# A state-space layer and a mixture-of-experts attention layer: gate products ahead of their Silus, sums with the newest state last, the first outputs further back

## The chip, the cores and the metric

The kernel is one program on one core of a Trainium2 chip. The metric is the device time of one execution in microseconds; the median of the runs counts. All times below that are places in the execution are microseconds from the start of the profiled span.

The engines have short names in the profile. PE is the matmul engine, with PEld its weight loads. DVE is the vector engine, ACT the scalar engine, POOL the GpSimd engine and SP the engine that issues most transfers. Each engine works through its own instructions in the order in which the program put them there; an instruction that waits holds up all behind it on that engine.

## The reference

The input is x with 8 sequences of 512 tokens and 256 features, in float32. Two layers follow one another, each as `x + layernorm(layer(layernorm(x)))`.

The first layer is a state-space layer (Mamba) with 512 inner channels and 16 states per channel:

```python
xz = x @ in_proj_w.T
x_ssm, z = jnp.split(xz, 2, axis=-1)
xc = silu(causal_conv(x_ssm, conv_w) + conv_b)      # 4 taps per channel
xp = xc @ x_proj_w.T                                # 1 + 16 + 16 columns
dt = softplus(dt_r @ dt_proj_w.T + dt_proj_b)
h = dA_t * h + dBx_t                                # a scan over the 512 tokens
y = einsum('bdn,bn->bd', h, C_t)                    # summed over the 16 states
return (y + xc * D) * silu(z) @ out_proj_w.T
```

The second layer is an attention with 16 heads of 64 features, in which the values and the outputs of every head are sums over 8 experts. A sigmoid gate per head and expert keeps the best two of the eight. A feed-forward part with 1024 hidden features and two layer norms follow:

```python
v = einsum('bsd,bhse,hedp->bhsp', x, gate(x, Wsel_v), Wv)
att = softmax(q @ k.T / 8)                          # q, k with rotary angles
o = einsum('bhst,bhtp->bhsp', att, v)
src2 = einsum('bhsp,bhse,hepd->bsd', o, gate(x, Wsel_o), Wo)
```

## The kernel before

**Names.** b is the sequence (0 to 7), a pair is two heads, so there are eight pairs (0 to 7) per sequence. The page's line numbers are those of the file; all DVE instructions stand at L175, because a helper issues them, so they are told apart by the names of their tiles.

**Order.** PE, DVE, ACT and POOL take their instructions in the order in which the Python code emits them (L1274); SP's transfers are placed by the framework. The code decides this order with a small planner, `_Order` (L98-162). It keeps a clock `now` for PE, which `pe(us)` moves on by a declared cost, and a clock `vec` for DVE. `after(us, do)` puts a piece of work in a queue with a due time. Background routines are generators: each `yield wait` says when the routine may go on, and a part of one is emitted when DVE has room in the plan. `order_of.run()` emits all that is due by `now`, and `order_of.run(until)` moves the clock on until a condition holds. So the declared costs set the order of the instructions but not their times.

**The routines.** `front(b)` does the input side of the state-space layer of sequence b: norm, input projection, convolution, Silu, the projection to step size and states, the gate silu(z), which is kept in DRAM (`sz_d`). `mamba(b)` does the scan and the output side, and then the gates of the attention's values (`best(0, gv)`); at the end it starts `heads(b)`, which does the gates of the outputs (`best(1, gt)`), turns them on PE into `ps_go`, copies them, stores them in `go_d` and adds b to the set `gated` (L781-795). `feed_forward(b)` is what follows the attention.

**The scan.** A step k (0 to 31) treats two of the 16 states (NG = 2) for 128 of the 512 channels (block m = k mod 4). DVE makes a scan over 2 x 512 elements and then the product of h with ct, the C coefficients. ACT computes the decay `da` for step k + 1 during step k. From step 4 of sequence 0 on, PE makes the scan's inputs as matmuls with diagonal matrices, in a PSUM tile `ps_u`; those for step k + 1 are emitted at step k (L643). POOL adds the products to `xc` by accumulating transfers, two per step (`add`, L570). The last four steps of sequence 0 are added by PE instead: `add_last` (L578) sums the two states of h and xc in PSUM with the identity as weights, and DVE multiplies two blocks at a time with the gate (L673). The number of the step last begun is kept in `at["step"]`.

**The second front.** `front(1)` runs during the scan of sequence 0. When step 8 (2 x NC) has begun it emits two gate products, `ps_in_g` and `ps_in` (L401, L402), each with its weight transfer on SP, then the Silus of xs, then the Silus and stores of the two gates (L404, L411), and 2.2 us later the state projection `ps_x`. The two products lie in PSUM until ACT has read them.

**The attention.** `ahead(n, following)` (L1257) emits PE's order for a pair n, mixed with the outputs of the pair before it. "v0" is a value product (`values`, two token blocks for one head), "s0" a block of scores (`scores`), "t0" the turning of a softmax block (`turn_over`), a number is an output product of the pair before (`add_output`), and `following` the next pair's projection to q and k. Behind a value product DVE forms ve, with the gates, and POOL sums over experts. Behind scores DVE takes the maximum (low), ACT the exponentials, DVE a reciprocal (total), and ACT scales. Value products, scores and turned blocks take three PSUM buffers in turn (`banks`, L282).

`attend` (L939) multiplies softmax and values, copies the result to `o`, and asks for the first two output gates 0.8 and 0.9 us later in the plan (`weigh_soon`, L956): if b is in `gated`, `weigh` is called, else it asks again 0.5 us later. `weigh` (L963) issues the transfers of the gate rows (`gb`, from `go_d`) on SP and the product og on DVE. There are two buffers each for gb and og. Output products k = 2q and 2q + 1 read og q; after the second one, `weigh(q + 2)` is emitted (L1006).

Of the kernel before, what the change touches and what calls it, by code (L numbers as in the profile page):

```python
# [37 lines left out]
NC = DI // P  # L38
NG = 2
# [58 lines left out]
class _Order:  # L98
# [11 lines left out]
    def pe(self, us):  # L110
        self.now += us
        self.here = self.now
# [4 lines left out]
    def after(self, us, do):  # L117

        heapq.heappush(self.queue, (self.here + us, self.n, do))
        self.n += 1  # L120
# [95 lines left out]
def _layers(  # L216
# [4 lines left out]
    with ExitStack() as ctx:  # L221
# [8 lines left out]
        step = pool("step", 2)  # L230
# [51 lines left out]
        def banks(name):  # L282
            return psum.tile([P, 2, S], F32, tag="mm", name=name)
# [14 lines left out]
        n = NT * 2 * H  # L298
        steps = NS // NG * NC

        at = dict(step=-1)
        state = {}
        pe, after, then = order_of.pe, order_of.after, order_of.then

        def front(b):
# [34 lines left out]
            def project(m, ps=None):  # L340

                w = wpool.tile([P, ND, 2 * P], F32, tag="w_m", name=f"w_in_{b}_{m}")
                nc.sync.dma_start(out=w, in_=m_in[:, :, m * P : (m + 2) * P])
                ps = banks(f"ps_in_{b}_{m}") if ps is None else ps
                for i in range(2):
                    for c in range(ND):
                        nc.tensor.matmul(  # L347
                            ps[:, i, :], lhsT=w[:, c, bass.ts(i, P)], rhs=xt[:, c, :],
                            start=(c == 0), stop=(c == ND - 1),
                        )  # L350
                pe(3.42)
                return ps
# [24 lines left out]
            for m in range(NC):  # L377
# [7 lines left out]
                for k in range(KC - 1):  # L385
                    yield 0.0
                    late = KC - 1 - k
# [7 lines left out]
                    states(px, range(2))  # L395
                    pe(1.71)
            yield free(0.1)
            while b == 1 and at["step"] < 2 * NC:
                yield Free(0.5)
            if b == 1:  # L400
                gates = [project(NC, psum_a.tile([P, 2, S], F32, tag="sum", name="ps_in_g"))]  # L401
                gates.append(project(NC + 2))  # L402
            for xc in xs if b else xs[1:]:
                nc.scalar.activation(xc, xc, AF.Silu)  # L404
            if b == 0:
# [66 lines left out]
            for u in us:  # L472
                m = 2 * len(lns)
# [11 lines left out]
            for ln, u in zip(lns, us):  # L485
                m = 2 * lns.index(ln)
# [13 lines left out]
        def mamba(b):  # L500
# [67 lines left out]
            xc = one.tile([P, NC, S], F32, tag="xc", name=f"xc_{b}")  # L568
# [9 lines left out]
            def add_last(k):  # L578

                m, h = k % NC, hs[k]  # L580
                if m % 2 == 0:
                    last.append(
                        banks("ps_y") if m else psum_a.tile([P, 2, S], F32, tag="sum", name="ps_y_0")
                    )
                terms = [h[:, j, :] for j in range(NG)] + [xc[:, m, :]]
                for i, a in enumerate(terms):
                    nc.tensor.matmul(
                        last[-1][:, m % 2, :], lhsT=ident, rhs=a,
                        start=(i == 0), stop=(i == len(terms) - 1),
                    )  # L590
                pe(2.6)

            scanning.add(b)
            if b + 1 < B:
                if b:
                    order_of.start(front(b + 1), 2 * b - 1 if b > 1 else 2.5)
                order_of.start(mamba(b + 1), 2 * (b + 1))
# [5 lines left out]
            for k in range(steps):  # L603
                g, m = k // NC * NG, k % NC
# [12 lines left out]
                h = hs[k] = step.tile([P, NG, S], F32, tag="h", bufs=4, name=f"h_{b}_{k}")  # L617
# [30 lines left out]
                if k - 1 >= by_dma:  # L648
                    add_last(k - 1)
# [14 lines left out]
            if b:  # L664
                yield 5.2
                add(steps - 1, 1)
                yield 3.5
            else:
                add_last(steps - 1)
                yield 0.1  # L670
# [126 lines left out]
        class Pair:  # L797
# [155 lines left out]
                for q in range(E // 2 if self.final else 2):  # L953
                    after(0.8 + 0.1 * q, lambda q=q: self.weigh_soon(q))

            def weigh_soon(self, q):  # L956

                if self.b in gated:
                    self.weigh(q)
                else:  # L960
                    after(0.5, lambda: self.weigh_soon(q))

            def weigh(self, q):  # L963

# [292 lines left out]
        def ahead(n, following):  # L1257


            for part in (  # L1260
                "v0", "s0", 0, 1, "v1", "s1", 2, 3, "t0", "s2", "v2", "t1", "s3", following, 4,
                "v3", 5, "t2", 6, "t3", 7,
            ):
                if isinstance(part, int):
                    if last:
                        last.add_output(part)
                elif isinstance(part, str):
                    {"v": n.values, "s": n.scores, "t": n.turn_over}[part[0]](int(part[1]))
                else:
                    part()  # L1270
                order_of.run()

        last, net = None, last_net()
        with tc.manual_schedule(engines=MANUAL):  # L1274
            first = front(0)
            order_of.start(first, 0, next(first))
            order_of.start(mamba(0), 0)
            order_of.start(front(1), FIRST, 9.0)
            first_constants()
            order_of.run(lambda: 0 in scanning)  # L1280
            order_of.start(later_constants(), NET)
            load(0, 0)
            order_of.run(lambda: 0 in inputs_of)
            pairs = {}
            follow(-1, H // 2 - 1)
            for b in range(B):
                for pair in range(H // 2):
                    if (b, pair) == (B - 1, 1):
                        next(net)
                    now = pairs.pop((b, pair))  # L1290
                    load(*next_one(b, pair))
                    ahead(now, lambda: follow(b, pair))
                    if pair == 0 and b:
                        order_of.start(feed_forward(b - 1, sums[b - 1]), NET)
                    now.attend()
                    order_of.run()
                    last = now
            order_of.run(lambda: not order_of.rest)
            next(net, None)
# [83 lines left out]
```

## Time and profile before

| what | us |
|---|---|
| median of 3 runs (lowest to highest) | 3668.6 (3666.76 to 3671.24) |
| the profiled execution's own time | 3673.76 |
| its span, first to last instruction | 3672.0 |
| PE busy (11250 matmuls) | 3406.9 (93%) |
| DVE busy | 3048.9 (83%) |
| ACT busy | 1664.0 (45%) |
| POOL busy | 1677.5 (46%) |
| mean granted PE clock, share of full | 0.97 |

The page divides the span into 40 slices of 91.8 us; a digit is the busy share of one slice in tenths, and PEclk is the PE clock that was granted. In the timeline a row is a start, a duration, the engine, the line, the operation, what it writes and reads, shapes and count; the bracket at the end gives how long the engine stood idle before it and what released it. Rows of like instructions are merged, so a row's duration can hold gaps. Some matmul records are missing from a trace.

### The profile page before, as it was taken

How to read it: one execution, taken by the hardware profiler on the slowest of the kernel's cores; microseconds unless marked ns; L12 is line 12 of the kernel's file. 1: busy time of each engine (PE TensorE's matmuls, PEld its weight loads, DVE VectorE, ACT ScalarE, POOL GpSimd, SP SyncE). 2: the span in 40 equal slices, each digit the busy share in tenths (PEclk: the TensorE clock that was granted, in tenths of full speed). 3: DMA queues.
4: the chain of work that ended last, by engine and by line, in shares of the span. 5: the costliest groups of instructions: out<-in, count | busy, mean ns of one | idle time of the engine just before them, and what ended most of it. 6: DMA issues, size and time to landing. Idle time of an engine off the chain costs nothing.

```text
span 3672.0 us, 35171 instructions
## 1 busy us (share of the span) xinstructions
PE 3406.9 (93%) x11250; PEld 1678.2 (46%) x11250; DVE 3048.9 (83%) x3198; ACT 1664.0 (45%) x2866; POOL 1677.5 (46%) x1597
## 2 busy tenths in 40 slices
PE   5768989989899999999999999999999999999997
PEld 3533334444344444444444444445444444446555
DVE  7878898799989898999989998899988999654443
ACT  5624443545543455344644446444553444332332
POOL 1425663354645545354454555355443657232321
PEclk8879999999999999999999999999999999999999
DMA  4927774577866768577755868568765778443430
GB/s 136 198 73 175 179 173 115 150 181 176 196 144 165 176 169 195 124 182 181 197 139 143 203 154 204 146 154 188 183 171 128 181 186 203 118 126 92 115 106 26
DMA packets 282534, 574.06 MB, mean 156 GB/s; under 512 B 37224, under 2 KB 124520, under 8 KB 282096
## 3 DMA queue, kind: packets, MB, share of 16 engines
q1 hardware_dynamic: 201584, 422.88, 40.0%
q0 software_dynamic: 80768, 148.95, 24.3%
q8 instruction: 91, 1.49, 0.2%
q14 instruction: 91, 0.75, 0.1%
HBM read 403.36 MB, written 19.42 MB: 115 GB/s over the span
## 4 chain that ended last, share of the span: by engine, by line
PE 48%; DVE 27%; issue 8%; DMA 7%; ACT 5%; POOL 5%; SPq 0%; DVEq 0%; POOLq 0%; ACTq 0%
PE ps_v L916 14%; DVE h L175 11%; PE ps_a L1000 9%; DMA xc<-h 5%; PE ps_qk L819 5%; PE ps_s L857 4%; PE ps_a L1020 3%; PE ps_o L946 3%; PE ps_pt L892 3%; DVE ve L175 2%; DVE og L175 2%; DVE low L175 2%; DVE xs L175 2%; PE ps_in L347 1%; DVE hit L175 1%
## 5 line engine op out<-in xcount | busy, mean ns | idle before, releaser
L916 PE MATMUL ps_v<-wv,xt 128*128 128x512 f32 x2048 | 945.8, 605 | 20.4 <-DVE y L175 13.3
L932 POOL TENSOR_TENSOR ve<-ve 128x512 f32<-128x512 f32 x256 | 423.6, 1655 | 1148.1 <-DVE ve L175 996.5
L1000 PE MATMUL ps_a<-og,wo 128*128 128x512 f32 x1792 | 847.1, 606 | 28.0 <-DVE og L175 27.7
L872 ACT ACTIVATE p<-ps_s,low 128x512 f32<-128x512 f32 x512 | 347.3, 683 | 723.0 <-DVE low L175 722.6
L574 POOL DMA_DIRECT2D xc<-h x504 | 463.8, 1099 | 382.1 <-DMA xc<-h 170.0
L916 PEld LDWEIGHTS ps_v<-wv,xt 128*128 128x128 f32 x2048 | 385.9, 193 | 536.9 <-issue 481.3
L175 DVE TENSOR_TENSOR_SCAN h<-da,h 128x1024 f32<-128x1024 f32 x228 | 541.2, 2374 | 10.3 <-ACT da L511 0.4
L1000 PEld LDWEIGHTS ps_a<-og,wo 128*128 128x128 f32 x1792 | 326.5, 192 | 440.9 <-issue 371.4
L881 ACT ACTIVATE p<-p,total 128x512 f32<-128x512 f32 x512 | 341.5, 714 | 252.2 <-DVE total L175 251.4
L175 DVE TENSOR_TENSOR og<-o,gb 128x1024 f32<-128x1024 f32 x256 | 320.1, 1271 | 128.8 <-ACT o L952 81.6
L175 DVE TENSOR_TENSOR ve<-ps_v,gv 128x1024 f32<-128x1024 f32 x256 | 311.7, 1218 | 130.0 <-PE ps_v L916 102.7
L898 ACT COPY pt<-ps_pt 128x1024 f32<-128x1024 f32 x256 | 256.9, 1005 | 347.3 <-PE ps_pt L892 345.9
L511 ACT ACTIVATE da<-dt,decay 128x511 f32<-128x511 f32 x512 | 339.8, 714 | 103.9 <-DVE h L175 100.8
L175 DVE TENSOR_TENSOR h<-bt,dtx 128x1024 f32<-128x1024 f32 x228 | 321.2, 1409 | 34.6 <-DMA xc<-h 34.4
L175 DVE TENSOR_TENSOR h<-h,ct 128x1024 f32<-128x1024 f32 x256 | 338.0, 1320 | 3.8
L175 DVE TENSOR_REDUCE low<-ps_s 128x2 f32<-128x1024 f32 x256 | 310.8, 1214 | 26.8 <-PE ps_s L857 26.1
L933 POOL TENSOR_TENSOR ve<-ve 128x256 f32<-128x256 f32 x256 | 318.1, 1243 | 20.1
L841 POOL DMA_DIRECT2D qk<-sin x256 | 204.5, 1209 | 256.7 <-DVE qk L175 128.9
L857 PE MATMUL ps_s<-qk 64*128 64x512 f32 x1024 | 295.0, 650 | 24.3 <-ACT p L872 14.0
L892 PEld LDWEIGHTS ps_pt<-ident,p 128*128 128x128 f32 x2048 | 239.4, 141 | 124.1 <-issue 87.1
L946 PE MATMUL ps_o<-pt,v 128*64 128x512 f32 x1024 | 249.9, 615 | 30.8 <-POOL v L934 16.7
L892 PE MATMUL ps_pt<-ident,p 128*128 128x128 f32 x2048 | 266.8, 274 | 6.4 <-ACT pt L898 2.6
(165 smaller groups left out, 3579.0 us busy)
## 6 DMA issues: line engine op xcount, KB each, us to landing
gb<-go_d SPq DMA_DIRECT2D x512, 256.0 KB, 4.8
xc<-h POOLq DMA_DIRECT2D x504, 256.0 KB, 5.6
wv<-in_wv_dram SPq DMA_DIRECT2D x128, 512.0 KB, 5.9
wo<-in_wo_dram SPq DMA_DIRECT2D x504, 128.0 KB, 4.0
ct<-bc_d SPq DMA_DIRECT2D x64, 512.0 KB, 5.8
bt<-bc_d SPq DMA_DIRECT2D x57, 512.0 KB, 5.6
wqk<-in_wqk_dram SPq DMA_DIRECT2D x64, 256.0 KB, 2.7
qk<-sin POOLq DMA_DIRECT2D x256, 64.0 KB, 4.8
```

The costliest lines, as they stand in the source:

```text
L175: return getattr(self.engine, name)(*args, **kw)
L511: nc.scalar.activation(das[k % 2][:, j, 1:S], dt[:, m, 1:S], AF.Exp, scale=decay[:, m, g + j : g + j + 1],)
L574: nc.gpsimd.dma_start(out=xc[:, k % NC, :], in_=hs[k][:, j, :], accum_op=ALU.add)
L857: nc.tensor.matmul(ps[:, j, :], lhsT=self.qk[feats, 0, bass.ts(t, P)], rhs=self.qk[feats, 1, :], start=True, stop=True,)
L872: nc.scalar.activation(p[:, j, :], ps[:, j, :], AF.Exp, bias=low[:, j : j + 1], accum_out=total[:, j : j + 1],)
L881: nc.scalar.mul(p[:, j, :], p[:, j, :], total[:, j : j + 1])
L892: nc.tensor.transpose(pp[:, j, bass.ts(i, P)], self.p[t][:, j, bass.ts(i, P)], ident)
L916: nc.tensor.matmul(ps[:, i, :], lhsT=self.xt[:, c, bass.ts(t + i, P)], rhs=self.wv[:, c, :], start=(c == 0), stop=(c == ND - 1),)
L932: nc.gpsimd.tensor_tensor(ve[:, :, 0:4], ve[:, :, 0:4], ve[:, :, 4:8], ALU.add)
L933: nc.gpsimd.tensor_tensor(ve[:, :, 0:2], ve[:, :, 0:2], ve[:, :, 2:4], ALU.add)
L946: nc.tensor.matmul(po[j * HP : j * HP + HP, 0, :], lhsT=self.v[:, j, t, :], rhs=self.pt[:, j, t, :], start=(t == 0), stop=(t == NT - 1),)
L1000: nc.tensor.matmul(pa[:, c, :], lhsT=self.wo[:, i, bass.ts(c, P)], rhs=self.og[q][:, i, :], start=(self.pair == 0 and k == 0), stop=(self. ...
```

## The change

There are three edits, all effective near the start of the program.

1. In `front(1)` the two gate products are emitted when step 7 has begun, and the Silus wait until step 9 has begun.
2. In `add_last` the term xc is summed first and the two states of h after it.
3. For pair 1 of sequence 0, whose outputs are those of pair 0, PE's order is v0 s0 v1 s1 t0, then outputs 0 and 1, and then s2 v2, outputs 2 and 3, t1 s3. The other pairs keep their order. And `weigh_soon`, where it had to ask more than once, puts `weigh` into the plan 6.0 us after the gates are there.

```diff
@@ front
-            while b == 1 and at["step"] < 2 * NC:
+            while b == 1 and at["step"] < 2 * NC - 1:
                 yield Free(0.5)
             if b == 1:
                 gates = [project(NC, psum_a.tile([P, 2, S], F32, tag="sum", name="ps_in_g"))]
                 gates.append(project(NC + 2))
+                while at["step"] < 2 * NC + 1:
+                    yield Free(0.5)
             for xc in xs if b else xs[1:]:
                 nc.scalar.activation(xc, xc, AF.Silu)
@@ add_last
-                terms = [h[:, j, :] for j in range(NG)] + [xc[:, m, :]]
+                terms = [xc[:, m, :]] + [h[:, j, :] for j in range(NG)]
@@ weigh_soon
-            def weigh_soon(self, q):
+            def weigh_soon(self, q, late=False):
                 if self.b in gated:
-                    self.weigh(q)
+                    after(6.0 if late else 0.0, lambda: self.weigh(q))
                 else:
-                    after(0.5, lambda: self.weigh_soon(q))
+                    after(0.5, lambda: self.weigh_soon(q, True))
@@ ahead
-            for part in (
+            usual = (
                 "v0", "s0", 0, 1, "v1", "s1", 2, 3, "t0", "s2", "v2", "t1", "s3", following, 4,
                 "v3", 5, "t2", 6, "t3", 7,
-            ):
+            )
+            second = (
+                "v0", "s0", "v1", "s1", "t0", 0, 1, "s2", "v2", 2, 3, "t1", "s3", following, 4,
+                "v3", 5, "t2", 6, "t3", 7,
+            )
+            for part in second if (n.b, n.pair) == (0, 1) else usual:
```

## Prediction

> **What bounds the kernel now.** I read the page's slices first, then the waits of DVE and PE, then the timeline around the three places that the change touches.
>
> ```profile
> PE   5768989989899999999999999999999999999997
> DVE  7878898799989898999989998899988999654443
> PEclk8879999999999999999999999999999999999999
> ```
>
> A slice is 91.8 us. From the fourth on PE is nine tenths busy, and DVE nearly so until the last ones. Only the first three (to 275 us) have slack: there the scan of batch 0 runs on DVE. All three edits lie before 335 us. After that the program order is the old one (shown below), so a microsecond won or lost there is carried to the end; nothing later waits for a fixed time.
>
> **Part 1: the gate products (L398-411).** Timeline before:
>
> ```profile
> 93.36 4.02 PE L549 MATMUL ps_u<-diag,dtx_t 128*128 128x128 f32 x20 [2.23 <-ACT diag L539]
> 97.21 3.60 PE L347 MATMUL ps_in_g<-xt_m,w_in 128*128 128x512 f32 x8
> ...
> 104.28 1.02 ACT L364 ACTIVATE sz<-ps_in 128x1024 f32<-128x1024 f32 x1 [2.41 <-PE ps_in L347]
> ...
> 107.98 2.29 DVE L175 TENSOR_TENSOR_SCAN h<-da,ps_u 128x1024 f32<-128x1024 f32 x1 [4.71 <-ACT da L511]
> ```
>
> Scan 10 waits 4.71 us for its decay (da), which stands on ACT behind two table loads, four Silus and ACT's waits for the products (0.49 + 2.41). The change gives the products to PE behind the inputs of scan 8, and the Silus to ACT behind the decay of scan 10. ACT's 2.9 us of waiting go. But PE is in order: the inputs of scan 9 now stand behind 16 matmuls. They start at 94.2 (the last four of scan 8's inputs, from 93.36 at 0.21 each). The granted clock, read in stretches of half a microsecond, was 0.50 from 89.7 to 96.56, then 1.00. So 2.36 us at 0.86 each make 2.7 of them, and 13.3 at 0.43 take 5.7: done at 102.3. The inputs of scan 9 (16 at 0.11) end at 104.05, and scan 9, which ran at 99.74, starts at 104.1. **The stall moves from scan 10 to scan 9.** On: scan 9 to 106.4, product to 107.6, scan 10 to 109.9, product to 111.0. ACT: Silus from 100.6, over at 105.95, table 1.28, decay 11 at 108.6. PE: inputs 10 to 105.8, state projection (3.43) to 109.4, inputs 11 to 111.3. Scan 11 at 111.35 against 111.66: gain 0.3. With the clock at 1.00 throughout it would be 1.4 better on PE, with another 3.4 us at 0.50 some 1.7 worse: +-1.5. SP: the weights of the products are loaded by 45 us, so their moved DMAs cost nothing; the two stores of sz move by about 3 us and are read at 176 us. The PSUM bank of the second product is free (105.95) before the state projection takes it.
>
> **Part 2: the last states' sums (L585).** The tail of that scan:
>
> ```profile
> 187.03 2.29 DVE L175 TENSOR_TENSOR_SCAN h<-da,ps_u 128x1024 f32<-128x1024 f32 x1 [4.21 <-DMA xc<-h]
> ...
> 190.72 3.75 PE L587 MATMUL ps_y<-h,ident 128*128 128x512 f32 x4 [4.10 <-DVE h L175]
> ...
> 194.27 1.67 PE L587 MATMUL ps_y<-xc,ident 128*128 128x512 f32 x2
> 195.77 1.88 PE L587 MATMUL ps_y<-h,ident 128*128 128x512 f32 x4
> 197.49 1.02 PE L587 MATMUL ps_y<-xc,ident 128*128 128x512 f32 x2
> 198.35 1.03 PE L684 MATMUL ps_out<-w_out,xc 128*128 128x256 f32 x4
> 198.55 1.23 DVE L175 TENSOR_TENSOR xc<-ps_y,sz 128x1024 f32<-128x1024 f32 x1 [3.38 <-PE ps_y L587]
> ```
>
> With xc first, the new order waits at its head for xc's DMA adds. They are there: scan 30 at 187.03 and scan 31 at 190.50 could write their buffers only when those adds had landed. So xc of state 30 runs at 187.05, in PE's idle 4.1 us. The stop in the middle of that idle time then keeps the clock up: in this trace PE's clock fell to 0.50 at 188.73 after a stretch of 3.4 us with 38% busy, and stayed at 1.00 over one with 49% (311.6 to 315.0). Here the stretch has 55%. Then h of state 30: 190.72 to 192.6, xc of state 31 to 193.5, and h of state 31, whose product ends at 194.04, to 196.0. The DVE product follows at 196.1 against 198.55: gain 2.4. With the clock at 0.50 as before it is 1.2. I take 2.3. The chain behind it is serial to 250 us (output projection, norm, gates), so it passes on.
>
> **Part 3: the second pair.** The stall that the change is aimed at:
>
> ```profile
> 284.58 1.13 PE L857 MATMUL ps_s<-qk 64*128 64x512 f32 x4
> 285.61 9.57 SPq L970 DMA_DIRECT2D gb<-go_d  x8
> 290.66 1.23 DVE L175 TENSOR_TENSOR og<-o,gb 128x1024 f32<-128x1024 f32 x1 [8.00 <-DMA gb<-go_d]
> 291.94 6.67 PE L1000 MATMUL ps_a<-og,wo 128*128 128x512 f32 x8 [6.23 <-DVE og L175]
> 292.85 1.23 DVE L175 TENSOR_TENSOR og<-o,gb 128x1024 f32<-128x1024 f32 x1 [0.96 <-DMA gb<-go_d]
> ...
> 295.12 1.22 DVE L175 TENSOR_TENSOR ve<-ps_v,gv 128x1024 f32<-128x1024 f32 x1
> ```
>
> DVE stands 8.0 us at the first og, whose gate rows land at 290.6, and PE 6.2 us behind it. Two edits bear on it. The 6.0 us in weigh_soon (L956) apply only where the gates were not ready at the first ask. The first ask comes 0.8 after attend's end in the plan (L954). The gates (L781-795) are a part that falls due 0.6 before that end by the declared costs; it then costs 0.6 + 0.05. So gated at +0.65, asked at +0.80: **late stays false**, og is put on DVE where it was, and DVE still stands until 290.66. Parts 1 and 2 shift this plan as a whole. In the trace ps_go (280.56) does run ahead of the second pair's first value product (281.05).
>
> What is left is PE's order v0 s0 v1 s1 t0, outputs 0 1, s2 v2, outputs 2 3, t1 s3. v1 fills 285.7 to 289.2. Then s1 needs the PSUM buffer of v0 (three, in turn), which DVE's ve frees, and ve stands behind og. The first pair, which has this order, shows that wait:
>
> ```profile
> 250.57 2.08 PE L857 MATMUL ps_s<-qk 64*128 64x512 f32 x4 [2.73 <-DVE ve L175]
> ```
>
> ve ends at 296.34; s1 runs to 298.6 (2.08, clock at 0.50). t0 needs the scaled p of s0: DVE low 296.26, h product 297.4, scan 298.9 to 301.5, ve of v1 to 302.7, reciprocal, then ACT's scaling 302.94 to 304.28. So t0 at 304.3 (1.97 at 0.50, as at 254.97). PE idles 7.3 + 5.7 us where it idled 6.2. Outputs 0 and 1 follow at 306.3. [...]
>
> Now DVE: low of s1, h product to 305.2, then og 2, which needs the buffer that outputs 0 and 1 read: it waits to 311.8, 6.5 us. Behind it queue the reciprocal, low 2 and scan 3. PE: s2 to 312.8, v2 316.2, outputs 2 3 to 319.6, t1 320.5, s3 321.6, next pair's qk at 321.6 against 316.46. DVE reaches scan 4 at about 323.5 against 318.61. From there both orders are the old ones, each 4.9 to 5.1 later. [...] SP: wo of output 4 waits for output 1, now 311.8 for 298.4, lands 4 us later, and is needed at 325; what is behind it (wv, gb, bt) has its user after 337. POOL's order changes only by its ve adds.
>
> **Sum.** -0.3 - 2.3 + 5.1 = +2.5 us. The profiled execution took 3673.76 around a span of 3672.0 (1.76 outside); its 5 us above the median 3668.6 are its own. The difference goes on the median: **3671.1**, own range 3667 to 3676.
>
> **Rivals.** *The gates come late after all* (0.18). Then ve, low, h product and scan 2 run before 290.66, s1's buffer is free at 286.2, and t0 starts at about 296.6 instead of 304.3: 7.7 less, so -2.6 + 5.1 - 7.7 = -5.2, and -7 if the clock is up again a stretch earlier: 3662. For it: DVE's 8.0 us are there to be had. Against it: the 0.15 in the plan. *Another step of the scan gets in front of the reciprocal* (0.30). The place is DVE between ve 0 and total of s0; an h product and scan cost 1.14 + 2.6 = 3.7, and t0, outputs, og 2 and all behind move by it; with part 1's bad end (1.5) the sum is 2.5 + 3.7 + 1.5 = 7.7: 3676.3, to 3680 if the product of v1 costs twice. It decides from about 4.8 us of DVE work added there. For it: DVE is busy 49.36 us of the 50 from 300. Against it: low, one step, ve is all that falls due. *Change 1 does nothing but move the stall* is in my sum already.
>
> **Numbers.** 0.2%, 7.3 us, is about what a measurement of this kernel tells from no change. My case (0.52) gives 0.01 faster, 0.41 same, 0.10 slower; the gates late 0.13, 0.05, 0; the extra step 0, 0.08, 0.22. Together 0.14, 0.54, 0.32. The range takes in both rivals' centres: 3660 to 3680.
>
> **What would show it.** Right: scan 9 waits about 4.4 us for ps_u, scan 10 none; the second DVE product of ps_y at 2 us less behind scan 31; the first og still 8 us idle, s1 released by ve, t0 by ACT p, og 2 idle some 6 us behind ps_a, qk of the third pair 2 to 3 us later than 316.46. Wrong: ve ahead of the first og on DVE, with that idle time under 3 us; or an order after 335 us that differs from the old one.

## The result

Both kernels were run side by side, 20 times each. The kernel before had a median of 3673.35 us (3662.94 to 3681.96), the changed one 3678.17 us (3671.61 to 3685.21). The ratio is **1.0021, with a 95% interval of 1.0013 to 1.0028: 7.7 us slower, 4.8 to 10.3**. The forecast was 2.5 us slower. The sign is right and the loss was expected in the right place, but the sum is about 5 us short, and the interval lies above it. (The ratio is the larger of the readings: the two medians lie 4.8 us apart and the two means 6.1. All lie above the forecast.)

The profiled execution of the changed kernel has a span of 3675.7 us (3672.0 before). The slices of its page are those of before but for single tenths (PE 8 for 9 in the fifth slice, from 367 us; DVE one more in the fifth, the eighth and the 25th, one less in the 24th):

```profile
PE   5768889989899999999999999999999999999997
DVE  7878998899989898999989989899988999654443
PEclk8879999999999999999999999999999999999999
```

The fourth slice, in which the second pair lies, is the same to the tenth: a loss of this size is not to be read here, and the three places have to be looked at one by one. Line numbers after L403 are 2 or 3 higher than in the kernel before, and later ones up to 9.

**Part 1.** The timeline of the changed kernel, PE and DVE together (start, duration, engine, line, and in brackets the idle time ahead and what ended it):

```profile
94.56 4.73 PE L347 MATMUL ps_in_g<-xt_m,w_in 128*128 128x512 f32 x8
99.13 3.60 PE L347 MATMUL ps_in<-xt_m,w_in 128*128 128x512 f32 x8
...
104.61 2.29 DVE L175 TENSOR_TENSOR_SCAN h<-da,ps_u 128x1024 f32<-128x1024 f32 x1 [4.59 <-PE ps_u L551]
...
108.07 2.28 DVE L175 TENSOR_TENSOR_SCAN h<-da,ps_u 128x1024 f32<-128x1024 f32 x1
...
111.93 2.29 DVE L175 TENSOR_TENSOR_SCAN h<-da,ps_u 128x1024 f32<-128x1024 f32 x1 [0.32 <-PE ps_u L551]
```

The 4.71 us in front of scan 10 are gone, and 4.59 us stand in front of scan 9. Scan 11 starts at 111.93; before it was 111.66.

**Part 2.** The same view at the end of that scan:

```profile
186.32 1.10 PE L589 MATMUL ps_y<-xc,ident 128*128 128x512 f32 x2 [1.30 <-DMA xc<-h]
189.91 3.78 PE L589 MATMUL ps_y<-h,ident 128*128 128x512 f32 x4 [2.49 <-DVE h L175]
193.48 1.91 PE L589 MATMUL ps_y<-xc,ident 128*128 128x512 f32 x2
195.19 2.20 PE L589 MATMUL ps_y<-h,ident 128*128 128x512 f32 x4
...
197.43 1.22 DVE L175 TENSOR_TENSOR xc<-ps_y,sz 128x1024 f32<-128x1024 f32 x1 [2.98 <-PE ps_y L589]
```

The xc matmuls of state 30 do run in PE's idle time, after 1.30 us of waiting for the DMA adds. But the four h matmuls behind them still take 3.78 us, twice their 1.88 at full clock. The second product follows scan 31 (189.77) by 7.66 us, where it followed it by 8.05.

**Part 3.** The stall of the second pair:

```profile
290.21 1.22 DVE L175 TENSOR_TENSOR og<-o,gb 128x1024 f32<-128x1024 f32 x1 [7.64 <-DMA gb<-go_d]
...
295.93 2.08 PE L859 MATMUL ps_s<-qk 64*128 64x512 f32 x4 [6.68 <-DVE ve L175]
303.03 1.97 PE L894 MATMUL ps_pt<-ident,p 128*128 128x128 f32 x8 [5.02 <-ACT p L883]
304.79 5.43 PE L1003 MATMUL ps_a<-og,wo 128*128 128x512 f32 x8
...
310.25 1.22 DVE L175 TENSOR_TENSOR og<-o,gb 128x1024 f32<-128x1024 f32 x1 [5.67 <-PE ps_a L1003]
...
323.37 2.27 DVE L175 TENSOR_TENSOR_SCAN h<-da,h 128x1024 f32<-128x1024 f32 x1
...
347.32 2.84 PE L1003 MATMUL ps_a<-og,wo 128*128 128x512 f32 x6 [2.96 <-DVE og L175]
```

DVE stands idle for 7.64 us in front of the first og, as it did before (8.00); s1 waits for ve, t0 for p, and outputs 0 and 1, the DVE's og 2 behind them, come last. The scan that began at 318.61 begins at 323.37. The last line is a wait that the kernel before doesn't have. There the outputs of the next pair started without one:

```profile
341.84 3.70 PE L1000 MATMUL ps_a<-og,wo 128*128 128x512 f32 x8
```

### The profile page after: what moved, and what is told of

It reads as the page before. It is cut to its first block, busy times and chain, and to the rows that moved or that the text cites. A ratio compares the mean times of both kernels' runs of the same rounds, so it can differ in the third digit from the quotient of the medians.

```text
span 3675.7 us, 35178 instructions
## 1 busy us (share of the span) xinstructions
PE 3404.8 (93%) x11250; PEld 1678.5 (46%) x11250; DVE 3049.4 (83%) x3198; ACT 1664.2 (45%) x2866; POOL 1677.6 (46%) x1597
## 3 DMA queue, kind: packets, MB, share of 16 engines
q0 software_dynamic: 80768, 148.95, 24.3%
## 4 chain that ended last, share of the span: by engine, by line
PE 47%; DVE 27%; issue 8%; DMA 7%; ACT 5%; POOL 4%; SPq 0%; DVEq 0%; POOLq 0%; ACTq 0%
PE ps_v L918 14%; DVE h L175 11%; PE ps_a L1003 9%; PE ps_qk L821 5%; DMA xc<-h 4%; PE ps_s L859 4%; PE ps_a L1023 3%; PE ps_o L948 3%; PE ps_pt L894 2%; DVE og L175 2%; DVE low L175 2%; DVE ve L175 2%; DMA gb<-go_d 2%; PE ps_in L347 2%; DVE hit L175 1%
## 5 line engine op out<-in xcount | busy, mean ns | idle before, releaser
L1003 PE MATMUL ps_a<-og,wo 128*128 128x512 f32 x1792 | 844.7, 604 | 24.4 <-DVE og L175 24.3
L175 DVE TENSOR_TENSOR_SCAN h<-da,h 128x1024 f32<-128x1024 f32 x228 | 540.8, 2372 | 10.3 <-ACT da L513 0.4
L175 DVE TENSOR_TENSOR h<-bt,dtx 128x1024 f32<-128x1024 f32 x228 | 320.6, 1406 | 33.4 <-DMA xc<-h 33.2
L175 DVE TENSOR_REDUCE low<-ps_s 128x2 f32<-128x1024 f32 x256 | 310.4, 1213 | 26.8 <-PE ps_s L859 25.9
```

The lines of the kernel that those rows point to most:

```text
L175: return getattr(self.engine, name)(*args, **kw)
L1003: nc.tensor.matmul(pa[:, c, :], lhsT=self.wo[:, i, bass.ts(c, P)], rhs=self.og[q][:, i, :], start=(self.pair == 0 and k == 0), stop=(self. ...
```

## The experiments

A single execution differs from the next by several microseconds (the kernel before took 3662.94 to 3681.96), so two yardsticks are used: the ratio over five rounds, and distances inside a trace between two marks. "Scan 35" is the scan at 318.61 in the kernel before; its distance from the first og (290.66) is 27.95 us. Ratios are given as microseconds of 3670, with their 95% interval.

### Each part alone

Part 1 alone has only the first hunk of the diff:

```
-            while b == 1 and at["step"] < 2 * NC:
+            while b == 1 and at["step"] < 2 * NC - 1:
...
+                while at["step"] < 2 * NC + 1:
+                    yield Free(0.5)
```

> Part 1 alone: the gate products behind the inputs of scan 8, the Silus behind the decay of scan 10; nothing else changed. The prediction's step says -0.3 +- 1.5 us: scan 9 at about 104.5 behind ps_u (some 4.5 us), scan 10 without a wait, scan 11 within 0.5 us of 111.66. My theory after the two traces (the gain is nothing, the stall only moves): scan 11 at 111.7, total within 1.5 us of the kernel before. Rival, that the moved products are part of the loss (by the clock or by the stores of sz): total 2 us or more above the kernel before, and visible by 198 us as a second ps_y product later than 198.6.

Measured: +2.2 us (-1.8 to 6.2). Scan 9 waits 4.76 us for ps_u, scan 10 nothing, scan 11 is at 111.60. From scan 7 to scan 11 it is 19.1 us here; over all profiles it is 18.8 to 20.2 in the five without part 1 and 18.9 to 20.4 in the nine with it. **Part 1 moves the stall and gains nothing.** The rival's loss is not excluded by the time alone, but no later mark in the trace shows it: the second DVE product of `ps_y` ("the second product" from here on) is at 197.38, and not later than 198.6.

Part 2 alone has only the sums:

```
-                terms = [h[:, j, :] for j in range(NG)] + [xc[:, m, :]]
+                terms = [xc[:, m, :]] + [h[:, j, :] for j in range(NG)]
```

> Part 2 alone: xc first in the sums of the last states. The prediction's step says -2.3 us at the second ps_y product (196.2 for 198.55), carried to the end. My theory now: the xc product of state 30 waits for the last DMA add and starts at about 186.5 to 187, the stretch before it is idle so that the clock falls to 0.50 all the same, the second product is at 197.4 to 198.0, and by the first value product of the second pair (281 us) half of that is lost again; total 0 to -1.5 us. Rival (the prediction's step was right and part 1 spoils it in the changed kernel): second product at 196.2, clock 1.00 from 187 to 191, total -2.3.

Measured: +1.8 us (-1.8 to 5.5). The timeline of this kernel:

```profile
187.13 1.10 PE L587 MATMUL ps_y<-xc,ident 128*128 128x512 f32 x2 [1.02 <-DMA xc<-h]
190.72 3.78 PE L587 MATMUL ps_y<-h,ident 128*128 128x512 f32 x4 [2.49 <-DVE h L175]
...
198.19 1.22 DVE L175 TENSOR_TENSOR xc<-ps_y,sz 128x1024 f32<-128x1024 f32 x1 [2.92 <-PE ps_y L587]
```

The product is at 198.19 and the clock is down again, as in the changed kernel. So part 1 did not spoil it; the prediction's 196.2 does not come by itself.

Part 3 alone is the changed kernel without those two hunks:

> Part 3 alone: the second pair's order and the later weighing, without parts 1 and 2. The prediction's step says +5.1 us: og still 8 us idle on DVE, s1 behind ve at about 296.5, t0 behind p at 304, outputs 0 and 1 to 311.7, qk of the third pair at 320 to 321.6, the fourth scan at 323.5, and all of it carried: total +5.1. My theory now is the same, with up to 2 us more or less from what DVE's planner swaps between 301 and 582 us: total +4 to +7. Rival (the order costs little by itself, and the loss comes from the three parts together): total within 2 us of the kernel before.

Measured: **+5.5 us (1.5 to 9.2)**. Its timeline has the same four waits:

```profile
293.34 2.08 PE L857 MATMUL ps_s<-qk 64*128 64x512 f32 x4 [6.75 <-DVE ve L175]
300.44 1.97 PE L892 MATMUL ps_pt<-ident,p 128*128 128x128 f32 x8 [5.02 <-ACT p L881]
...
307.45 1.23 DVE L175 TENSOR_TENSOR og<-o,gb 128x1024 f32<-128x1024 f32 x1 [5.46 <-PE ps_a L1001]
...
320.58 2.27 DVE L175 TENSOR_TENSOR_SCAN h<-da,h 128x1024 f32<-128x1024 f32 x1
```

Scan 35 follows the first og (287.60) by 32.98 us, in the changed kernel by 33.17; in the five profiles with the old order it is 27.9 to 28.3. On the means of the two and the five that is 33.1 for 28.0, the loss of 5.1, and it is all in part 3. (The absolute times of this trace are 3 us early; that was so before part 3 began.)

Parts 1 and 2 without part 3 leave every pair in the usual order:

```
-            for part in second if (n.b, n.pair) == (0, 1) else usual:
+            for part in usual:
```

> Parts 1 and 2 without the second pair's order (every pair in the usual order). The prediction's sum says -2.6 us. My theory now: second ps_y product 1 us earlier, 0 to -0.5 left at 281 us, total 0 to -1.5. Rival, that parts 1 and 2 are themselves a loss: total +2 or more.

Measured: +0.4 us (-3.7 to 4.0). The second product follows scan 31 by 7.80 us. Parts 1 and 2 are neither a visible gain nor a visible loss; a gain of 2.6 is just inside the interval, so the traces have to say why it isn't there.

### Why the sums gain nothing

The view of stretches, cut into windows of 3.413 us, half the time from the clock's fall to its return (188.73 to 195.56 before, 188.99 to 195.82 after), that begin and end within 0.06 us of these changes, shows for the kernel before (stretch, its length, then busy time of PE, PE loads, DVE, ACT, POOL, and the granted clock third from the end):

```profile
185.37:188.78 3.41, 1.25 (x3) 0.19 (x1) 1.75 (x1) 0.88 (x1) 0.82 (x1) 0.99 1.08 347
188.78:192.19 3.41, 1.47 (x2) 0.84 (x3) 3.38 (x3) 0.00 (x0) 0.00 (x0) 0.50 0.20 35
192.19:195.61 3.42, 3.42 (x5) 1.35 (x4) 2.94 (x3) 0.00 (x0) 0.00 (x0) 0.51 0.16 30
195.61:199.02 3.41, 3.41 (x11) 1.72 (x9) 0.47 (x1) 0.00 (x0) 0.00 (x0) 1.00 0.36 129
```

and for the changed kernel:

```profile
185.64:189.05 3.41, 1.10 (x2) 0.30 (x2) 2.71 (x2) 0.00 (x0) 0.00 (x0) 0.99 0.94 281
189.05:192.46 3.41, 2.55 (x3) 1.18 (x4) 3.38 (x3) 0.00 (x0) 0.00 (x0) 0.50 0.01 1
192.46:195.87 3.41, 3.41 (x5) 1.35 (x4) 1.98 (x2) 0.00 (x0) 0.00 (x0) 0.51 0.36 141
195.87:199.29 3.42, 2.97 (x11) 1.68 (x10) 1.76 (x3) 0.00 (x0) 0.00 (x0) 1.00 0.06 18
```

PE is busy 1.25 of 3.41 us in the first stretch before (37%), 1.10 after (32%), and the clock falls at its end both times. It comes back after the stretch that is full (192.19, 192.46), not after the one with 2.55 busy (75%). From 60 to 440 us the changes of the clock lie on such a grid in all fourteen profiles (in these two none is more than 0.02 us off it). The grid lies differently in each execution: the fall at the end of that scan comes 1.8 us ahead of scan 31 in the kernel before and 0.9 us behind it in the one with part 3 alone. Wherever it lay, part 2 did not keep the clock up: in all eight profiles that have part 2 as it was changed, the clock fell between 1.3 us ahead of scan 31 and 1.3 us behind its start, after a window with PE 0.27 to 0.40 busy. If that is the cause, filling PE's idle time should keep the clock. The next kernel has part 2 and gives the xc term of state 30 four times; each but the last is thrown away by the restart of the sum:

```
+                terms = [xc[:, m, :]] * (4 if k == steps - 2 else 1) + [h[:, j, :] for j in range(NG)]
...
+                        start=(i < len(terms) - NG), stop=(i == len(terms) - 1 or i < len(terms) - 1 - NG),
```

> The kernel before with part 2 alone, and in the sum of state 30 the xc product given four times (each restarts the sum, so the result is the same): about 2.6 us more of work in PE's idle time while scan 30 runs. Theory: the granted clock is set on a grid of 3.41 us that lies anew in every execution, falls after a stretch with less than about 0.47 of PE busy and comes back only after one with more than about 0.82; the changed kernel's xc product made that stretch only 0.32 busy, so the clock fell. With the four it is over 0.6 busy, the clock stays at 1.00, and the second ps_y product follows scan 31 by 5.4 to 5.8 us (7.2 to 8.0 in the kernels before, 7.6 to 7.8 with part 2 alone): the 2.4 us of the prediction's step. Rival: the product is held by DVE and not by the clock; then it follows by 7 us or more with the clock at 1.00. Total: -1 to -2.5 if the gain survives the stages to 281 us, 0 if the next idle time takes it.

Its stretches, cut at the grid of its own later fall and, below them, DVE's scan 31 and second product:

```profile
185.20:188.60 3.40, 2.55 (x6) 0.77 (x5) 0.00 (x0) 3.02 (x3) 0.87 (x1) 1.00 1.08 303
188.60:192.00 3.40, 3.27 (x8) 1.44 (x8) 3.25 (x2) 0.00 (x0) 0.00 (x0) 1.00 0.84 243
192.00:195.40 3.40, 3.16 (x7) 1.06 (x6) 3.37 (x3) 0.00 (x0) 0.00 (x0) 1.00 0.00 0
```

```profile
192.18 2.28 DVE L175 TENSOR_TENSOR_SCAN h<-da,ps_u 128x1024 f32<-128x1024 f32 x1
...
197.79 1.22 DVE L175 TENSOR_TENSOR xc<-ps_y,sz 128x1024 f32<-128x1024 f32 x1 [0.94 <-PE ps_y L587]
```

**The clock stays at 1.00 and the second product follows scan 31 by 5.61 us**: 2.4 less than in the profile of the kernel before, the very size that the prediction gave part 2 (1.6 to 2.4 less than in the four profiles without part 2, which lie between 7.2 and 8.05). The rival, that DVE holds it, falls. The whole run is -0.7 us (-4.0 to 2.6), which can't tell a gain of 2 from none.

The changed kernel has two matmuls of 0.43 us less behind state 30 (two took the 0.86 us from 197.49 to 198.35 in the trace of before, at full clock). Why do these 0.86 us not arrive? A first part is missing at the second product already: it follows scan 31 by 6.4 to 7.8 us in the eight profiles with part 2, by 7.2 to 8.05 in the four without, and the means are only 0.1 apart. Then the next stage waits for the same grid. Its selection matmuls, in the kernel before

```profile
222.86 5.39 PE L720 MATMUL ps_sel<-w_sel,xt 128*128 128x256 f32 x16 [1.10 <-ACT xt L713]
```

and in the changed kernel

```profile
221.73 6.08 PE L722 MATMUL ps_sel<-w_sel,xt 128*128 128x256 f32 x16 [1.10 <-ACT xt L715]
```

start 1.1 us earlier and take 0.7 longer, because the clock comes back at 226.28 in one and 226.54 in the other. All fourteen profiles agree: the selection matmuls always start 24.3 us behind the second product, and DVE's `key`, which waits for them, starts 29.7 to 31.0 us behind it, the later the later the clock comes back (27.6 to 30.2). From the second product to the first og it is 91.8 to 92.3 us in the four profiles without part 2 and 92.5 to 93.3 in the eight with it: 0.9 us are handed back. How they divide among the stages behind `key` was not taken apart. From scan 31 to the first og the means are 99.5 without part 2 and 100.3 with it, in ranges that overlap.

### Which piece of the order costs

The later weighing made effective (it was meant for late gates; in the trace above og stands where it stood):

```
-                    after(6.0 if late else 0.0, lambda: self.weigh(q))
+                    after(6.0 if (self.b, self.pair) == (0, 0) else 0.0, lambda: self.weigh(q))
```

> The changed kernel with its later weighing made effective: the 6.0 apply to the first pair of batch 0 whether or not its gates were ready at the first ask. This is the prediction's first rival. On DVE the h product and scan of the next step, ve and low now stand ahead of the first og. Expected by that rival: the first og waits under 3 us, s1 starts at 289 to 290 without waiting for ve, t0 at 295 to 297 for 303, qk of the third pair at 313 for 320.2; total about 7 us under the changed kernel, 1 to 2 under the kernel before. If instead it is the order of PE itself that costs the 5 us (outputs late, og 2 behind them), the idle time only moves: qk of the third pair at 318 or later and the total within 2 us of the changed kernel.

Measured: -0.4 us (-4.0 to 3.3), about 8 under the changed kernel. The first og waits 0.94 us, s1 starts at 287.35 behind v1, t0 at 295.38, qk at 312.05; scan 35 follows the first og by 24.4 us for 33.2. The rival of the prediction is right about what it would have been worth; the kernel as changed doesn't do it.

Only v1 ahead of outputs 0 and 1, in the changed kernel:

```
-                "v0", "s0", "v1", "s1", "t0", 0, 1, "s2", "v2", 2, 3, "t1", "s3", following, 4,
+                "v0", "s0", "v1", 0, 1, "s1", 2, 3, "t0", "s2", "v2", "t1", "s3", following, 4,
```

> The changed kernel with another order of the second pair on PE: v0 s0 v1, outputs 0 and 1, s1, outputs 2 and 3, t0, s2, v2, t1, s3; only v1 is moved ahead of the first outputs. If the loss comes from putting s1 and t0 (which wait for ve and p on DVE and ACT) ahead of the outputs, this order must lose nothing: outputs 0 and 1 at 292 as in the kernel before, og 2 without a long wait, qk of the third pair at 314 to 316.5 (v1's 3.7 us now in time that was idle), total 0 to 3 us under the kernel before. If the loss comes from moving the value product ahead (its PSUM buffer, its ve on DVE), qk stays at 319 or later and the total at +4 or more.

Measured: -1.8 us (-5.1 to 1.5); scan 35 at 28.2 us. No loss, but v1's 3.7 us are not won either, and qk (317.49, the first og at 291.64) is where the old order has it: 25.85 us behind the first og, 25.80 before. Further down v2 now waits for the PSUM buffer of s1:

```profile
309.65 5.40 PE L918 MATMUL ps_v<-wv,xt 128*128 128x512 f32 x8 [2.86 <-ACT p L874]
```

So moving the value product is not the cause. The last cut leaves s1 ahead of the outputs and puts t0 back behind them; outputs 2 and 3 then stand ahead of s2 and v2, as in the usual order:

```
-                "v0", "s0", "v1", "s1", "t0", 0, 1, "s2", "v2", 2, 3, "t1", "s3", following, 4,
+                "v0", "s0", "v1", "s1", 0, 1, 2, 3, "t0", "s2", "v2", "t1", "s3", following, 4,
```

> The changed kernel with only s1 ahead of outputs 0 to 3, t0 behind them: v0 s0 v1 s1, outputs 0 1 2 3, t0. It separates the two waits on PE that the order causes, s1 behind ve (6.7 us) and t0 behind p (5.0 us). The prediction's step put outputs 0 and 1 at the end of both. Without t0 ahead of them they start at about 298 and end at about 303, og 2 waits to 303, and the fourth scan follows the first og by 29 to 31 us (33.0 in the two runs with the whole order, 28.0 with the old one): total +1 to +4. If s1's wait alone costs it all, 33 and +5 to +8; if t0's does, 28 and within 2.

Measured: -4.0 us (-7.3 to -0.7). In its timeline

```profile
299.32 2.08 PE L859 MATMUL ps_s<-qk 64*128 64x512 f32 x4 [6.78 <-DVE ve L175]
301.33 8.91 PE L1003 MATMUL ps_a<-og,wo 128*128 128x512 f32 x16
...
307.89 1.74 DVE L175 TENSOR_TENSOR og<-o,gb 128x1024 f32<-128x1024 f32 x1
```

s1 still waits 6.78 us for ve, but the outputs come straight behind it, og 2 finds its buffer free, and scan 35 follows the first og by 26.1 us. **The loss hangs on t0 ahead of the outputs**: its wait for p keeps outputs 0 and 1 5.0 us longer, DVE's og 2 waits for them, and the scan behind og 2 with it. (Outputs 2 and 3 moved too, but og 2 does not wait for those. With the effective weighing, where s1 did not wait and t0 stood ahead, og 2 still waited 4.64 us.) My expectation put half of the loss on s1; none is there. The interval of this run lies just below zero, but its trace does not show that it beats the kernel before: at the seventh attention product (602.24 us before) it is 311.7 us behind the first og, where five profiles with the old order have 310.4 to 312.8: up to there nothing is won.

### Versions that beat both

The effective weighing with the usual order:

> The changed kernel with the effective later weighing (6.0 for the first pair of batch 0) and the usual order of the second pair. It separates delay and order: DVE does the next step's product and scan, ve and low in the 8 us in front of the first og, PE still idles behind s0. Expected: first og waits about 1 us, fourth scan 21 to 25 us behind it (28.0 with the usual order and no delay, 20.6 with delay and v1 moved), total 3 to 6 us under the kernel before. If the delay does nothing without v1 in the idle time, 26 to 28 us and a total as before.

Measured: -5.1 us (-8.8 to -1.8). The first og waits 1.02 us; PE still idles 6.29 us in front of the first outputs. The delay alone does it.

With v1 in that idle time as well:

> The order of the run before this (only v1 ahead of outputs 0 and 1) together with the effective later weighing (6.0 for the first pair of batch 0). DVE's 8 us behind the gate rows and PE's 6 us are both filled. Expected: first og waits under 3 us, outputs 0 and 1 from 292, qk of the third pair at 311 to 314 and the fourth scan (318.61 before) at 313 to 316; total 2 to 5 us under the kernel before. If DVE's work is merely shifted, qk at 316 and the total as before.

Measured: -6.6 us (-10.6 to -2.6). In its timeline

```profile
287.84 1.23 DVE L175 TENSOR_TENSOR og<-o,gb 128x1024 f32<-128x1024 f32 x1 [0.99 <-DMA gb<-go_d]
...
289.12 3.70 PE L1003 MATMUL ps_a<-og,wo 128*128 128x512 f32 x8 [2.61 <-DVE og L175]
...
308.48 2.27 DVE L175 TENSOR_TENSOR_SCAN h<-da,h 128x1024 f32<-128x1024 f32 x1
```

DVE's 8 us shrink to 1 and PE's 6 to 2.6. In this execution the clock does not fall here, and the outputs take 3.70 us for 6.67. That is not certain with every grid: in the last run below the clock fell at 290.79 in spite of a wait of only 2.59 us, and the same outputs took 5.16. Scan 35 is 20.6 us behind the first og.

The same on the kernel before, without parts 1 and 2:

> The effective later weighing with only v1 ahead of outputs 0 and 1, on the kernel before: neither the gates' move nor the sums' new order. If parts 1 and 2 are worth nothing, total as with them: 5 to 8 us under the kernel before, fourth scan 20.5 us behind the first og. If part 2's 0.9 us of matmuls count, 1 to 2 us more than the run with them (-6.6).

Measured: -7.3 us (-11.0 to -3.7), scan 35 at 20.6 us. Parts 1 and 2 add nothing to it.

And with parts 1 and 2 and the xc term four times:

> The effective later weighing with only v1 ahead of outputs 0 and 1, parts 1 and 2 as changed, and the xc product of state 30 given four times to keep the clock up. If the two gains add (each is a stretch of one serial chain): second ps_y product 5.4 to 5.8 us behind scan 31, fourth scan of batch 1 at 308 to 312, total 7 to 9 us under the kernel before (-6.6 without the four). If the gain at 198 us does not reach the end, -5 to -7.

Measured: **-9.9 us (-14.7 to -4.8), median 3662.08**, the best of all. The product follows scan 31 by 5.61 us, scan 35 the first og by 20.3. The intervals of the last three overlap, so that the two gains add is likely from the traces and not shown by the times.

## Why the prediction was wrong

- **Part 1, "gain 0.3": the mechanism is right, and the gain is nought.** Scan 9 was put at 104.1 and came at 104.61, its wait at 4.4 and was 4.59, scan 11 at 111.35 and came at 111.93 (111.60 with part 1 alone, 111.66 before). Nothing is won, which is inside the +-1.5 given.
- **Part 2, "keeps the clock up", "I take 2.3": this is the step that failed.** The stretch of 55% was laid where the clock had changed in the trace of before, as though the grid would lie there again, and counted the xc matmuls beside 1.02 us of the sum ahead of them, which in the changed kernel's execution had ended (185.02) before the stretch began (185.64). The stretch was 32% busy, and the clock fell. That was not bad luck with the grid: it fell in all eight profiles with part 2. The step also gave 1.2 should the clock fall; the two matmuls are worth 0.86, and 0.1 of it was measured on the means at the second product. "So it passes on" failed as well: up to the selection matmuls the chain is serial (24.3 us in every profile), but that stage ended the later the later the clock came back (`key` 29.7 to 31.0 us behind the second product, the clock 27.6 to 30.2). Of 2.3 us nothing arrived.
- **Part 3, "late stays false", 5.1 in the sum: right.** The og stood at the same place; s1 was put at 296.3 and came at 295.93, t0 at 304.3 and 303.03, the end of outputs 0 and 1 at 311.8 and 310.2, scan 35 at 323.5 and 323.37. The distance from og to scan 35 grew by 5.1 us (28.0 to 33.1). No run shows the 311.8 on which the 5.1 is built. What the traces show is the return of the clock: in the kernel before it came 6.0 us behind the start of these outputs (291.94 to 297.96), in the changed one 5.4 us behind t0 (303.03 to 308.46), both times after the rest of one window of the grid and all of the next; outputs 0 and 1 then took 5.43 us where they took 6.67.
- **"From there both orders are the old ones": wrong for DVE.** PE's order is the old one from qk, but DVE takes some ve, low and scans of the next pairs in another order; the 2.96 us at 347.32 are an og that now stands behind a scan. At the seventh attention product the loss has grown from 5.1 to 6.7 us (on the means 318.5 behind the first og with the new order for 311.8 with the old), and is 4.8 at the last one, where the five with the old order lie 8 us apart.
- **The sum.** It is short by part 2's 2.3, part 1's 0.3 and up to 1.6 that part 3 loses later. With nothing for part 1, nothing for part 2 and 5.1 to 6.7 for part 3 it is +5 to +7, inside the measured 4.8 to 10.3. The rival of the extra step, which had the right total (7.7), had the wrong mechanism: DVE put no more in front of the reciprocal than forecast. The rest between 6.7 and 7.7 is not resolved by these runs.

## What to carry to other kernels

Before an instruction is moved ahead of others on an in-order queue, ask what it waits for, and who waits for what is now behind it: here one transpose that waited 5 us for ACT kept the outputs, these kept a buffer, and the buffer kept DVE. Look first at the engine that has the stall: here DVE weighed too early, and delaying that alone was worth about 5 us, where the three reorderings of PE tried without it gave +5.5, -1.8 and -4.0. And where a stretch ends with the return of the clock, a gain shorter than the spacing of its changes (here 3.413 us) should not be counted on: here one of about 1 us was handed back.

## What was not expected of the hardware

In the fourteen profiles the granted clock changed on a grid of 3.413 us from 60 to 440 us, and which way it went at a window's end went with the share that PE had been busy in it. All 179 falls came after a window under 0.50 busy, and no window under 0.42 kept the clock (from 0.42 to 0.49 both were seen). All 193 rises came after a window with 0.82 or more; none of those at 0.75 to 0.81 won the clock back, and at 0.82 to 0.83 both were seen. The clock was lost after windows in which PE was not wholly idle, too: in the changed kernel's from 185.58 to 188.99, 0.32 busy, PE never idled for more than 1.6 us at a stretch (187.42 to 188.99). The shares have an error, because some matmul records are missing and ends are modelled. Seven windows near 240 us look 0.88 to 1.00 busy in the records and were followed by no rise; in the kernel before, two score matmuls there (239.77) show 1.89 us, where four took 2.08 at the same clock (250.57), so their modelled ends may hide idle time. The grid lay differently in each execution (the fall from 1.8 us ahead of scan 31 to 0.9 us behind it in the two named above), and the same instructions without part 2 (scan 31 to the second product) took 7.2 to 8.05 us.
